# Unordered list scatters and a shift for the block count in a routed expert kernel

## The chip, the cores and the metric

The kernel runs on one core of a Trainium2 chip. The time is device microseconds from one launch, the median of several runs; lower is better. Engines are named as the profile names them: PE (matmul, with PEld for its weight loads), DVE (vector), ACT (scalar activation), POOL (GpSimd) and SP (which issues most DMAs).

## The reference, cut to what matters

4096 tokens of width 512 (two batches of 2048) pass through a linear-attention block and then a mixture of experts, each with a layer norm ahead and a layer norm and residual behind.

```python
x = x + layernorm(attn(layernorm(x)))            # 16 heads, 4 key heads, elu+1 features
def moe(x):                                      # 32 experts, width 192, 8 per token
    scores = softmax(x @ wg.T)
    weights, idx = top_k(scores, 8)
    weights = weights / weights.sum(-1)
    # every (token, expert) entry, sorted by expert:
    h = silu(xs @ w1[e]) * (xs @ v1[e])
    return zeros.at[token].add((h @ w2[e]) * weight)
x = x + layernorm(moe(layernorm(x)))
```

All arithmetic is in float32. 4096 tokens with 8 experts each give 32768 entries.

## The kernel before, in words

**Attention.** For each batch, the keys of 16 token tiles of 128 are reduced to a key state (`keys_of`), and then four blocks of 512 tokens run through `attn_block`. A finished block leaves four token tiles in a waiting list; `finish_next` takes one of them at a time, in between the work of the following block (or of the keys of the second batch), so each tile's residual, norm and routing run beside later attention matmuls. The last four tiles have no attention behind them; they are finished by the loop at L643, just ahead of the experts.

**Routing, `route_tile`.** For one tile of 128 tokens it computes the expert scores, the best eight (`top`), their weights, and for each of the eight a position in the expert's list: `carry` holds how many entries each expert has so far. `tw` (three buffers) holds token number and weight for each entry, `pi` (three buffers) the eight positions. L202 to L208 then issue eight indirect DMAs from POOL, one for each k; each scatters 128 entries of 8 bytes into `list_d` in device memory, which has room for 4096 entries for each expert. Every entry's row is written once. The list was filled with empty entries before by `clear_lists`. The framework that orders the program sees eight writes of the whole of `list_d` and makes each wait for the one before it to land. 32 tiles make 256 such DMAs.

**Two rounds of experts.** The lists are cut into blocks of 128 entries. Round 1 (48 blocks, 24 pairs) is planned after seven of the eight attention blocks, from the lists as they stand after 24 tiles. Round 2 takes the rest, up to 120 pairs; of these 114 run here. `plan_round` computes, with some forty small DVE operations on all 128 partitions, which expert and block each slot of a round holds, reads the blocks of the list by indirect DMA on POOL (L356: one for round 1, two for round 2), transposes them on PE, and leaves token numbers (`tid`), weights (`wt`) and expert numbers (`load`). For round 2 the number of pairs, `half`, is counted at L269 to L274: an iota of even numbers on POOL (`ev_i`), a copy, a comparison with the total number of blocks, and a sum. Its two list reads are held behind the matmul and scatter-add of round 1's pair 16 on their engines.

**A pair of blocks.** `prepare` loads the two experts' weights by SP (three buffers each; a load is skipped where the buffer already holds that expert), gathers the 128 tokens of each block by an indirect DMA on POOL (`xg`, L679, four buffers), transposes them on PE (L685) and copies them out on DVE (L687). `run_pair` multiplies with the first weights (L698), applies silu on ACT (`hs`, L701) and the product on DVE (`hh`, L702), transposes (L710), copies (`hT`, L712), multiplies with the second weights (`py`, L715 and L719), scales by the entry's weight on ACT into `ysb` (L723, three buffers), and adds the rows to `acc_d` by an indirect scatter-add on POOL (L724).

**What sets the order.** Every engine runs its own instruction list in order. The lists are written at build time by the framework's planner, which simulates the program and places an instruction when its inputs are ready; only SP keeps the order of the source in the expert rounds. A wait holds everything behind it on that engine. At the end, 16 steps add the two halves of `acc_d`, normalise, add the residual and store.

Of the kernel before, what the change touches and what calls it, by code (L numbers as in the profile page):

```python
# [9 lines left out]
I32 = mybir.dt.int32  # L10
U32 = mybir.dt.uint32
AF = mybir.ActivationFunctionType
ALU = mybir.AluOpType
AX = mybir.AxisListType
# [3 lines left out]
P = 128  # L18
# [5 lines left out]
def linear_attention_then_moe(  # L24
# [15 lines left out]
    nc = tc.nc  # L40
# [47 lines left out]
    list_d = dram.tile([E * CAP + BS, 2], F32, name="list_d")  # L88
# [30 lines left out]
    rn = ctx.enter_context(tc.tile_pool(name="rn", bufs=3))  # L119
# [7 lines left out]
    def transpose_rows(psum, dst, src):  # L127

        pt = psum.tile([P, C, P], F32, tag="pt", name="pt")
        for c in range(C):  # L130
            nc.tensor.transpose(pt[:, c, :], src[:, c * P : (c + 1) * P], ident)
        nc.vector.tensor_copy(dst, pt)
# [9 lines left out]
        return mv, rs  # L142

    carry = [None]

    def route_tile(i, xn):

        xnT = rn.tile([P, C, P], F32, tag="rn", name="xnT")
        transpose_rows(ps_r, xnT, xn)
        pl = ps_r.tile([P, E], F32, tag="pt", name="pl")  # L150
        for c in range(C):
            nc.tensor.matmul(pl, xnT[:, c, :], wg_sb[:, c, :], start=(c == 0), stop=(c == C - 1))
        nmx = sm.tile([P, 1], F32, tag="nmx", name="nmx")
        nc.vector.tensor_reduce(nmx, pl, AX.X, ALU.max, negate=True)
        sc = sm.tile([P, E], F32, tag="sc", name="sc")
        ssum = sm.tile([P, 1], F32, tag="ssum", name="ssum")
        nc.scalar.activation(sc, pl, AF.Exp, bias=nmx, accum_out=ssum)
        nc.vector.reciprocal(ssum, ssum)
        nc.vector.tensor_scalar_mul(sc, sc, ssum)

        top = sm.tile([P, K], F32, tag="top", name="top")
        nc.vector.max(top, sc)
        ti = sm.tile([P, K], U32, tag="ti", name="ti")
        nc.vector.max_index(ti, top, sc)
        e8 = sm.tile([P, K], F32, tag="e8", name="e8")
        nc.vector.tensor_copy(e8, ti)
        mk = sm.tile([P, E], F32, tag="mk", name="mk")
        nc.vector.match_replace(mk, top, sc, -1.0)
        nc.vector.tensor_single_scalar(mk, mk, 0.0, ALU.is_lt)

        pr = ps_r.tile([P, 2, E], F32, tag="pt", name="pr")
        nc.tensor.matmul(pr[:, 0, :], tri, mk, start=True, stop=True)
        nc.tensor.matmul(pr[:, 1, :], ones, mk, start=True, stop=True)

        tsum = sm.tile([P, 1], F32, tag="tsum", name="tsum")
        nc.vector.tensor_reduce(tsum, top, AX.X, ALU.add)
        nc.vector.reciprocal(tsum, tsum)
        tw = sm.tile([P, K, 2], F32, tag="tw", name="tw")
        nc.vector.tensor_copy(tw[:, :, 0], tok[:, i : i + 1].to_broadcast([P, K]))
        nc.vector.tensor_scalar_mul(tw[:, :, 1], top, tsum)  # L180

        before = ebase if carry[0] is None else carry[0]
        pos = sm.tile([P, E], F32, tag="pos", name="pos")
        nc.vector.tensor_add(pos, before, pr[:, 0, :])
        after = cy.tile([P, E], F32, tag="carry", name="after")
        nc.vector.tensor_add(after, before, pr[:, 1, :])
        carry[0] = after


        oh = sm.tile([P, K, E], F32, tag="oh", name="oh", bufs=2)  # L190
        nc.vector.tensor_tensor(
            oh,
            eidx.unsqueeze(1).to_broadcast([P, K, E]),
            e8.unsqueeze(2).to_broadcast([P, K, E]),
            ALU.is_equal,
        )
        nc.vector.tensor_mul(oh, oh, pos.unsqueeze(1).to_broadcast([P, K, E]))
        pos8 = sm.tile([P, K], F32, tag="pos8", name="pos8")
        nc.vector.tensor_reduce(pos8, oh, AX.X, ALU.add)
        pi = sm.tile([P, K], I32, tag="pi", name="pi")  # L200
        nc.vector.tensor_copy(pi, pos8)  # L201
        for k in range(K):  # L202
            nc.gpsimd.indirect_dma_start(  # L203
                out=list_d[:, :],
                out_offset=bass.IndirectOffsetOnAxis(ap=pi[:, k : k + 1], axis=0),
                in_=tw[:, k, :],
                in_offset=None,
            )  # L208

    def finish_tile(i, x1):  # L210

        rows = slice(i * P, (i + 1) * P)
        xr = rio.tile([P, HID], F32, tag="xr", name="xr")
        nc.sync.dma_start(xr, x[rows, :])
        nc.vector.tensor_add(x1, x1, xr)
        nc.sync.dma_start(x1_d[rows, :], x1)
        mv, rs = ln_stats(sm, x1)
        xn = rn.tile([P, HID], F32, tag="rn", name="xn")
        nc.vector.tensor_scalar(xn, x1, mv[:, 0:1], rs, ALU.subtract, ALU.mult)
        nc.sync.dma_start(xn_d[rows, :], xn)  # L220
        route_tile(i, xn)
# [32 lines left out]
    def plan_round(pool, nblk, offs, npair, gp, fixed, later=()):  # L254
# [6 lines left out]
        t = lambda name, w=ng: pool.tile([P, w], F32, name=name)  # L261
        incl = running_sum(pool, "incl", nblk)
        total = incl[:, E - 1 : E]
        half = t("half", 1)
        if fixed:
            assert fixed % 2 == 0
            nc.vector.memset(half, fixed / 2.0)
        else:
            evens = t("evens", npair)  # L269
            ev_i = rn.tile([P, npair], I32, tag="rn", name="ev_i")  # L270
            nc.gpsimd.iota(ev_i, [[2, npair]], base=0, channel_multiplier=0)
            nc.vector.tensor_copy(evens, ev_i)
            nc.vector.tensor_tensor(evens, evens, total.to_broadcast([P, npair]), ALU.is_lt)
            nc.vector.tensor_reduce(half, evens, AX.X, ALU.add)  # L274


        sec = t("sec", 1)
# [72 lines left out]
        lists = list_d.rearrange("(r f) o -> r (f o)", f=BS)  # L350
# [2 lines left out]
            order.enter_context(tc.issue_after(ins.ins))  # L353
        for g in range(ng):
            bl = rn.tile([P, BS, 2], F32, tag="rn", name="bl")
            nc.gpsimd.indirect_dma_start(  # L356
                out=bl[:n2].rearrange("p f o -> p (f o)"),
                out_offset=None,
                in_=lists,
                in_offset=bass.IndirectOffsetOnAxis(ap=row_i[:n2, g : g + 1], axis=0),  # L360
            )
            bt = rn.tile([P, 3, BS], F32, tag="rn", name="bt")
            nc.vector.tensor_copy(bt[:n2, :2, :], bl[:n2].rearrange("p f o -> p o f"))
            nc.vector.tensor_copy(bt[:n2, 2, :], ew[:n2, g : g + 1].to_broadcast([n2, P]))
            pt = ps_r.tile([P, 3, P], F32, tag="pt", name="pid")
            for o in range(3):
                nc.tensor.transpose(pt[:, o, :n2], bt[:n2, o, :], ident[:n2, :n2])
            nc.vector.tensor_copy(tid[:, g, :], pt[:, 0, :n2])
            nc.vector.tensor_copy(wt[:, g, :], pt[:, 1, :n2])
            nc.vector.tensor_copy(load[:, g, :], pt[:1, 2, :n2])  # L370
# [6 lines left out]
    with ExitStack() as actx:  # L377
# [243 lines left out]
        for b in range(B):  # L621
            acc = finish_kv(*keys)
            ms = fold_wo(acc)
            for t in range(NBLK):
                mid = attn_block(b, t, xls[t], acc, ms)
                if b == 0:
                    with tc.issue_after(mid):
                        clear_accumulators(t)
                if b * NBLK + t == SNAP:
                    nc.vector.tensor_sub(cnt1, carry[0], ebase)  # L630
                    full = blocks_of(route, "full", cnt1, BS - 1)
                    upto = running_sum(route, "upto", full)

                    f1 = route.tile([P, E], F32, name="f1")
                    nc.vector.tensor_sub(f1, full, upto)
                    nc.vector.tensor_scalar(f1, f1, float(N1), 0.0, ALU.add, ALU.max)
                    nc.vector.tensor_tensor(f1, f1, full, ALU.min)
                    round1 = plan_round(route, f1, None, NP1, NP1, N1)
            if b + 1 < B:
                keys = key_state()  # L640
                xls = keys_of(b + 1, *keys, lambda *_: finish_next())
# [5 lines left out]
    with ExitStack() as mctx:  # L647
# [90 lines left out]
        nblk = blocks_of(plan, "nblk", cnt, 0)  # L738
        nc.vector.tensor_sub(nblk, nblk, f1)
        round2 = plan_round(plan, nblk, f1, NP2, GP2, None, done[2 * NP1 // 3])  # L740
        np2 = plan.tile([P, 1], I32, name="np2")
        nc.vector.tensor_copy(np2, round2[3])
# [25 lines left out]
        for i in range(0, NTILE, 2):  # L768
            rows = slice(i * P, (i + 2) * P)
# [60 lines left out]
```

## Time and profile before

| | us |
|---|---|
| median of 3 runs | 2855.16 (2854.49 to 2856.72) |
| the profiled execution | 2861.29 |
| its span, first to last instruction | 2859.5 |
| attention, with the routing of 28 tiles | 0 to about 1335 |
| round 1, with the routing of the last four tiles | about 1335 to 1660 |
| round 2 | to about 2765 |
| closing norm and stores | to 2859.5 |

| engine | busy us | share |
|---|---|---|
| PE | 2645.8 | 93% |
| DVE | 1061.4 | 37% |
| POOL | 1059.9 | 37% |
| ACT | 674.8 | 24% |

A row of a timeline gives the start, the length, the engine, the line, the operation and its tiles, how many instructions were merged, and in brackets how long the engine had been idle and what ended that. "issue" means that the profile shows no wait. Busy time of POOL at a DMA is the time in which it prepares the transfer, not the transfer. A matmul's length follows the granted clock, which the rows by stretch give as a share of full speed.

The 256 list scatters (L203) keep POOL busy for 252.2 us, 985 ns each; POOL waits 365.8 us in 207 of them for the DMA of the scatter before.

### The profile page before, as it was taken

Reading aid. Unit: us, or ns where it says so; the run is one execution under the profiler, and the core shown is the slowest. Engines: PE = TensorE matmul, PEld = TensorE weight load, DVE = VectorE, ACT = ScalarE, POOL = GpSimd, SP = SyncE. Lnnn points to the kernel's source line nnn. Section 1 sums busy time; section 2 is a strip of 40 time slices with the busy share of each in tenths; the row PEclk is TensorE's granted clock in tenths of the full one; section 3 lists DMA queues with packets and bytes.
Section 4 is the critical chain, followed back from the end, with each engine's and each line's share of the span. In section 5 each row is a group of like instructions: output and inputs, shape, how many; then the busy total and the mean of one; then the engine's idle time right before and its main releaser. Section 6 shows DMA issues by size and latency. Waiting matters only on the chain. (4 is left out here: it accounts for less than half of the span.)

```text
span 2859.5 us, 29618 instructions
## 1 busy us (share of the span) xinstructions
PE 2645.8 (93%) x8443; PEld 1310.7 (46%) x8443; DVE 1061.4 (37%) x2432; ACT 674.8 (24%) x1208; POOL 1059.9 (37%) x891
## 2 busy tenths in 40 slices
PE   8999999998999999998779899999999999999850
PEld 3434444444444444444435455555555555555420
DVE  5334544546533536554412222222222222222217
ACT  4332222213331313221211112121212121212114
POOL 1100223122320122223455555555555555554426
PEclk9999999999999999999889999999999999999985
DMA  3291211212111212123647899989787988685548
GB/s 112 86 329 51 68 52 52 68 52 67 37 56 45 71 34 71 53 71 114 161 102 175 212 268 257 274 200 254 165 214 160 314 194 199 137 194 114 104 87 323
DMA packets 179290, 399.83 MB, mean 140 GB/s; under 512 B 29413, under 2 KB 30438, under 8 KB 178610
## 3 DMA queue, kind: packets, MB, share of 16 engines
q0 software_dynamic: 70144, 145.31, 25.1%
q1 hardware_dynamic: 101602, 237.55, 24.9%
q10 hardware_dynamic: 7376, 15.02, 1.4%
q8 instruction: 70, 1.15, 0.2%
q14 instruction: 98, 0.80, 0.1%
HBM read 488.74 MB, written 116.66 MB: 212 GB/s over the span
## 5 line engine op out<-in xcount | busy, mean ns | idle before, releaser
L698 PE MATMUL pgu<-w1t,xgT 128*128 128x384 f32 x2208 | 780.0, 496 | 3.5 <-issue 2.4
L724 POOL DMA_INDIRECT acc_d<-ysb,tid x276 | 441.9, 1601 | 503.8 <-ACT ysb L723 389.5
L203 POOL DMA_INDIRECT list_d<-tw,pi x256 | 252.2, 985 | 979.6 <-DVE pi L201 556.2
L698 PEld LDWEIGHTS pgu<-w1t,xgT 128*128 128x128 f32 x2208 | 399.5, 191 | 327.2 <-issue 109.3
L552 PE MATMUL pq<-xlT,wq_sb 128*128 128x512 f32 x1024 | 463.1, 598 | 1.2 <-DVE sq L559 1.2
L584 PE MATMUL acc<-m,sq 128*128 128x512 f32 x1024 | 463.0, 597 | 0.0
L702 DVE TENSOR_TENSOR hh<-hs,pgu 128x192 f32<-128x192 f32 x276 | 97.3, 355 | 975.9 <-ACT hs L701 838.2
L723 ACT ACTIVATE ysb<-py,wt 128x512 f32<-128x512 f32 x276 | 176.5, 684 | 783.4 <-PE py L719 731.8
L679 POOL DMA_INDIRECT xg<-xn_d,tid x276 | 274.9, 996 | 119.0 <-PE px L685 64.0
L552 PEld LDWEIGHTS pq<-xlT,wq_sb 128*128 128x128 f32 x1024 | 190.7, 190 | 241.5 <-issue 230.8
L584 PEld LDWEIGHTS acc<-m,sq 128*128 128x128 f32 x1024 | 189.1, 190 | 239.6 <-issue 239.1
L715 PE MATMUL py<-w2t,hT 128*128 128x512 f32 x552 | 266.4, 605 | 2.1 <-issue 2.1
L555 ACT ACTIVATE qe<-pq,nbq_sb 128x512 f32<-128x512 f32 x128 | 87.8, 686 | 514.6 <-PE pq L552 509.0
L687 DVE COPY xgT<-px 128x512 f32<-128x512 f32 x276 | 188.3, 683 | 43.6 <-PE px L685 41.3
L559 DVE SCALAR_TENSOR_TENSOR sq<-pq,bq_sb,qe 128x512 f32<-128x512 f32 x128 | 95.8, 748 | 286.0 <-ACT qe L556 285.9
L685 PE MATMUL px<-ident,xg 128*128 128x128 f32 x1104 | 174.2, 284 | 29.1 <-DMA xg<-xn_d,tid 26.7
L701 ACT ACTIVATE hs<-pgu 128x192 f32<-128x192 f32 x276 | 90.3, 330 | 363.2 <-PE pgu L698 336.7
L685 PEld LDWEIGHTS px<-ident,xg 128*128 128x128 f32 x1104 | 135.9, 147 | 56.9 <-issue 32.0
L715 PEld LDWEIGHTS py<-w2t,hT 128*128 128x128 f32 x552 | 107.5, 196 | 109.2 <-issue 74.0
L719 PE MATMUL py<-w2t,hT 64*128 64x512 f32 x552 | 157.1, 642 | 0.0
L710 PE MATMUL ph<-ident,hh 128*128 128x128 f32 x414 | 100.5, 298 | 51.3 <-DVE hh L702 51.2
L469 PE MATMUL pk<-wk_sb,xlT 128*128 128x512 f32 x256 | 119.7, 607 | 0.0
(185 smaller groups left out, 1844.8 us busy)
## 6 DMA issues: line engine op xcount, KB each, us to landing
w1t<-in_wgu_dram SPq DMA_DIRECT2D x276, 768.0 KB
w2t<-in_w2r_dram SPq DMA_DIRECT2D x276, 256.0 KB
w2t<-in_w2r_dram SPq DMA_DIRECT2D x276, 128.0 KB
nb<-nr_d SPq DMA_DIRECT2D x128, 256.0 KB
acc_d<-zero SPq DMA_DIRECT2D x6, 2048.0 KB
xb<-in_x_dram SPq DMA_DIRECT2D x32, 256.0 KB
xr<-in_x_dram SPq DMA_DIRECT2D x32, 256.0 KB
wo<-in_woT_dram SPq DMA_DIRECT2D x32, 256.0 KB
```

The lines of the kernel that those rows point to most:

```text
L203: nc.gpsimd.indirect_dma_start(out=list_d[:, :], out_offset=bass.IndirectOffsetOnAxis(ap=pi[:, k : k + 1], axis=0), in_=tw[:, k, :], in_of ...
L469: nc.tensor.matmul(pk, xlT[:, c, :], wk_sb[:, c, :], start=(c == 0), stop=(c == C - 1))
L552: nc.tensor.matmul(pq, wq_sb[:, c, h * P : (h + 1) * P], xlT[:, c, :], start=(c == 0), stop=(c == C - 1))
L584: nc.tensor.matmul(pa[s], a[:, s * P : (s + 1) * P], ms[h], start=(h == 0), stop=(h == H - 1))
L679: nc.gpsimd.indirect_dma_start(out=xg, out_offset=None, in_=xsrc, in_offset=bass.IndirectOffsetOnAxis(ap=tid[:, c0 : c0 + 1], axis=0),)
L685: nc.tensor.transpose(px[:, c, :], xg[:, c * P : (c + 1) * P], ident)
L687: nc.vector.tensor_copy(xgT, px)
L698: nc.tensor.matmul(pgu, xgT[:, c, :], w1t[:, c * F2 : (c + 1) * F2], start=(c == 0), stop=(c == C - 1))
L715: nc.tensor.matmul(py[s], hT[:, 2 * s, :], w2b[s][r][:, 0, :], start=True, stop=False)
L719: mm = nc.tensor.matmul(py[s], hT[rows, 1, :], w2b[s][r][rows, 1, :], start=False, stop=True)
L723: nc.scalar.activation(ysb, py[s], AF.Copy, scale=wt[:, c0 : c0 + 1])
L724: sc = nc.gpsimd.indirect_dma_start(out=acc_d[s][:, :], out_offset=bass.IndirectOffsetOnAxis(ap=tid[:, c0 : c0 + 1], axis=0), in_=ysb, in_ ...
```

## The change

Two things are changed.

The scatters into `list_d` are declared free of order among each other: each one is put into a group, and dependencies on members of that group are taken off the next. The three reads of the lists (L356) get an explicit dependency on every scatter issued before them in the program: 192 for round 1's read, 256 for each of round 2's.

For round 2, `half` is computed as (total + 1) shifted right by one bit, by three DVE operations on one column, in place of the iota on POOL and three DVE operations on 120 columns.

```diff
     carry = [None]
+    entries = []
...
         for k in range(K):
-            nc.gpsimd.indirect_dma_start(
+            sc = nc.gpsimd.indirect_dma_start(
                 out=list_d[:, :],
                 out_offset=bass.IndirectOffsetOnAxis(ap=pi[:, k : k + 1], axis=0),
                 in_=tw[:, k, :],
                 in_offset=None,
             )
+
+            tc.declare_no_dep(sc.ins, group="lists", reason="rows of list_d are set once")
+            tc.add_to_no_dep_group("lists", sc.ins)
+            entries.append(sc.ins)
...
         else:
-            evens = t("evens", npair)
-            ev_i = rn.tile([P, npair], I32, tag="rn", name="ev_i")
-            nc.gpsimd.iota(ev_i, [[2, npair]], base=0, channel_multiplier=0)
-            nc.vector.tensor_copy(evens, ev_i)
-            nc.vector.tensor_tensor(evens, evens, total.to_broadcast([P, npair]), ALU.is_lt)
-            nc.vector.tensor_reduce(half, evens, AX.X, ALU.add)
+            up = pool.tile([P, 1], I32, name="up")
+            nc.vector.tensor_scalar_add(up, total, 1.0)
+            nc.vector.tensor_single_scalar(up, up, 1, ALU.logical_shift_right)
+            nc.vector.tensor_copy(half, up)
...
-            nc.gpsimd.indirect_dma_start(
+            rd = nc.gpsimd.indirect_dma_start(
                 out=bl[:n2].rearrange("p f o -> p (f o)"),
                 out_offset=None,
                 in_=lists,
                 in_offset=bass.IndirectOffsetOnAxis(ap=row_i[:n2, g : g + 1], axis=0),
             )
+            for sc in entries:
+                tc.add_manual_dep(
+                    rd.ins, sc.name,
+                    mybir.DependencyInfo(mybir.DependencyClass.Sync, mybir.DependencyReason.DATA),
+                    reason="reads the lists",
+                )
```

## The prediction

> **What bounds the kernel now.** The chain of work that ended last covers only the closing normalisation (its shares are all near 0%), so I did not start there. I read, in order: the stretches of busy time by engine, the waits of PE, the timelines of PE, ACT, POOL and DVE around 1340 to 1510 us. PE is the busy engine (93% of the span), so a microsecond is worth something only where PE idles.
>
> Busy time by stretch (length, PE, weight loads, DVE, ACT, POOL, granted clock, DMA share, GB/s):
>
> ```profile
> 1340.00:1384.50 44.50, 39.09 (x160) 24.53 (x161) 27.59 (x113) 17.25 (x29) 16.26 (x14) 0.86 0.87 276
> 1384.50:1412.60 28.10, 12.43 (x35) 6.06 (x34) 9.86 (x46) 1.92 (x4) 13.99 (x13) 0.70 0.44 102
> 1412.60:1506.20 93.60, 67.01 (x211) 37.21 (x209) 15.24 (x34) 11.32 (x25) 49.36 (x45) 0.84 0.53 116
> 1506.20:1584.00 77.80, 77.08 (x274) 41.83 (x275) 18.98 (x40) 15.07 (x31) 42.40 (x33) 0.98 0.72 157
> ```
>
> A pair is 35 matmul records. The last row is round 1 undisturbed: L710 of successive pairs starts at 1527.07, 1536.90, 1546.73 us on PE, 9.83 us a pair. The second row does one pair in 28.1 us, the third six in 93.6 (15.6 a pair). That is where the list scatters of the last four token tiles (32 of the 256) run among the pairs. Between the start-up and 1300 us PE's matmuls wait under two microseconds at a time, but for 6.28 us at the batch change, behind a busy DVE.
>
> What holds the pairs, on POOL's timeline (start, length, idle before and releaser):
>
> ```profile
> 1413.37 0.98 POOL L203 DMA_INDIRECT list_d<-tw,pi  x1 [0.30 <-issue]
> 1421.92 0.98 POOL L203 DMA_INDIRECT list_d<-tw,pi  x1 [7.57 <-DMA list_d<-tw,pi]
> 1423.21 0.98 POOL L679 DMA_INDIRECT xg<-xn_d,tid  x1 [0.31 <-PE px L685]
> 1424.49 0.96 POOL L679 DMA_INDIRECT xg<-xn_d,tid  x1 [0.30 <-issue]
> 1425.75 1.00 POOL L203 DMA_INDIRECT list_d<-tw,pi  x1 [0.30 <-issue]
> 1428.56 0.97 POOL L203 DMA_INDIRECT list_d<-tw,pi  x1 [1.81 <-DMA list_d<-tw,pi]
> 1429.84 1.61 POOL L724 DMA_INDIRECT acc_d<-ysb,tid  x1 [0.30 <-issue]
> 1431.76 1.58 POOL L724 DMA_INDIRECT acc_d<-ysb,tid  x1 [0.30 <-issue]
> ```
>
> Each scatter waits for the scatter before it to land, here 7.57 and 1.81 us, and the in-order engine holds everything behind it. The scatter-add issued at 1429.84 had its data on ACT at 1419.21. ACT pays, then PE:
>
> ```profile
> 1427.78 0.69 ACT L723 ACTIVATE ysb<-py,wt 128x512 f32<-128x512 f32 x1 [4.78 <-PE py L719]
> 1435.03 0.69 ACT L723 ACTIVATE ysb<-py,wt 128x512 f32<-128x512 f32 x1 [6.56 <-DMA acc_d<-ysb,tid]
> 1435.61 0.54 ACT L701 ACTIVATE hs<-pgu 128x192 f32<-128x192 f32 x2
> ```
>
> ```profile
> 1427.68 4.78 PE L698 MATMUL pgu<-w1t,xgT 128*128 128x384 f32 x14
> 1436.38 0.47 PE L710 MATMUL ph<-ident,hh 128*128 128x128 f32 x1 [3.92 <-DVE hh L702]
> ```
>
> There are three ysb buffers, so the second copy of a pair needs the first scatter-add of the pair before to have landed (1429.84 to 1435.03, 5.2 us). Hence `hs`, `hh` and PE are late. At 1384 us there is a second form, on DVE:
>
> ```profile
> 1398.22 0.22 DVE L272 CAST evens<-ev_i 128x120 f32<-128x120 int32 x1 [13.44 <-POOL ev_i L271]
> 1398.36 0.35 DVE L702 TENSOR_TENSOR hh<-hs,pgu 128x192 f32<-128x192 f32 x1
> 1400.69 0.17 DVE L179 COPY tw<-tok 128x8 f32<-128x8 f32 x1 [1.99 <-DMA list_d<-tw,pi]
> ```
>
> The iota of round 2's plan sits on POOL behind scatters; DVE waits 13.44 us for it, with the pair's `hh` behind it, and PE idles 13.31.
>
> **Scatters without order.** Removed: the landing wait ahead of a scatter. Where nothing intervenes one scatter follows another every 2.37 us (0.97 busy, 1.40 wait); POOL's gathers, which do not wait for each other, follow every 1.27 (0.97 and 0.30). So 32 scatters cost 32 x 1.27 = 41 us of POOL, in bursts of eight (10.2 us), as each tile's `pi` is ready: 1359.8, 1370.6, 1377.6 us by the DVE timeline, the last near 1384. They can be over near 1404 us instead of 1501.9.
>
> *Six pairs, 1412.6 to 1506.2.* POOL then carries per pair two gathers (2 x 1.27) and two scatter-adds (2 x 1.91): 6.4 of 9.83 us. 93.6 - 6 x 9.83 = **34.6 us**.
>
> *The pair from 1384.4 to 1412.6.* It took 28.2, 18.4 over 9.83. How much returns depends on where the third scatter-add (first of the second pair, on ACT done by 1379.4) falls among the bursts, which the build decides and the trace cannot show. With none ahead: 18.4. With one burst, the first pair's two scatter-adds, then two bursts (1360.1 + 10.2 + 3.8 + 20.3): it issues at 1394.4, lands at 1399.6, while the copy that needs it would come at 1390.4: 9.2 late, of which some 2.5 us are slack (`hh` at 1420.45, `ph` at 1422.47 in the next, undisturbed pair, and 0.87 idle on ACT), so PE stalls 6.7. With three bursts it issues at 1404.6: a 17 us stall. With all four ahead even of the first scatter-add, the second copy of the pair before (1380.8) waits until some 1406: about 9 us worse than now. Ends: -9 and +18.4. I take two bursts, since the first scatter-adds become ready just as the first burst ends, and the third not until two more bursts are waiting.
>
> A stall also costs clock. After the 13.31 us wait `ph` x2 took 0.69 against 0.44, `pgu` x2 1.62 against 0.88, `py` 3.62 against 1.88 and 1.32 against 1.13: 2.9 us. [...] I take the row: 18.4 - 6.7 - 2.9 = **8.8 us**.
>
> [...] Then a burst would cost POOL next to nothing, and the sum would be 34.6 + 18.4 = 53. The 256 rows of 985 ns busy say otherwise; with them it is 43.4.
>
> *Elsewhere.* Token tiles beside attention: PE hides the scatters; DVE's `tw` waits of 3.2 and 3.7 us near 727 and 762 us each cost PE about 1.45, so 0 to 2.9. Against it, a burst may hold POOL's `sks` add for 10.2 us in the keys stage; `sk` has two buffers at about 7 us a tile, some 13 us of cover, 0 to -2. The first gathers of round 1 wait behind the last scatter at 1334.9, but attention's last matmuls also end there: 0 to 2. I take 0 for all three.
>
> **The shift.** Out: a POOL iota (0.24) and DVE's 0.22 + 0.28 + 0.28. In: three DVE operations on one column, 0.15 to 0.22 each by the plan's own one-column rows; the trace has no shift, but even doubled it is under 1.4 us. They hide beside PE as the plan's other thirty do. The 13.44 us wait goes, but alone it would buy little: next late is `tw` at 1400.69, whose buffer the first tile's scatters hold, and `hT` comes behind it in DVE's order. I count 0 beyond the sum above.
>
> **The wait on all scatters.** The list readers (L356) now name 192 or 256 scatters. At 17 ns for a semaphore row on POOL (x33 at L203) that is at most 4.4 us each, 8.8 for round 2's two; queued behind are the next pairs' gathers, and DVE's `bt`, which already holds `hh` for 9.23 us at 1593. At least it is 0, as all scatters have long landed. I take 0.1: the present reader also follows 256 scatters through one or a few semaphore values. That 7.4 us PE stall stays.
>
> **Sum.** 34.6 + 8.8 - 0.1 = 43.3 us. Against the profiled execution, 2861.3 (span 2859.5 and 1.8 around it), this gives 2818; that execution lies 6.1 above the median of the runs, so I predict 2855.2 - 43.3, **2812 us**.
>
> **Rivals.**
> - *Clean order* (0.25): the scatter-adds slip between scatters, 53 us and perhaps 3 from the `tw` waits: 2800. For it: the order of before also mixes both kinds. Against: eight scatters become ready at once.
> - *POOL becomes the bound for a while* (0.31): three or four bursts ahead of the scatter-adds, 34.6 - 1.3 to 34.6 - 9: 2822 to 2830.
> - *The waits do not go* (0.04), because another dependency keeps the order, or DVE's `tw` takes its place: the iota alone gives 0 to 2 us, 2854.
> - *Slower* (0.04): the scatters are put ahead of round 1's first gathers. These start at 1336.13; behind the fourth tile's burst they could start only near 1395, 59 us later with PE idle, against 53 recovered: 2861. It decides once the first gather starts after some 1389 us. Against: ten gathers stand ahead of these scatters today, since they are ready 24 us sooner.
>
> The likeliest case has 0.36. About 0.2% is what a measurement of this kernel can tell from no change: faster 0.92, within it 0.04, slower 0.04. The range takes in the first two rivals and the open terms: 2795 (53 + 2.9 + 2 + 2) to 2834 (34.6 - 9, less 4.4).
>
> **What would show it.** L203 spaced 1.27 us within a tile with no wait on its own DMA; the last scatter near 1404 us; no wait of ACT's ysb on acc_d of over 3 us after 1412; L710 every 9.83 us from then on; no evens row. PE's remaining stall before 1412 says which order was built. I am wrong if pairs stay above 10 us after the scatters end (then landing, not POOL, held them), or if attention grows.

## The result, and the profile after

The changed kernel takes 2883.4 us (median of 4 runs, 2873.8 to 2886.7) beside 2854.9 for the kernel before: a ratio of 1.0093, 95% interval 1.008 to 1.0107. It is slower by 0.9%, where 1.5% faster was forecast. The profiled execution has a span of 2884.8 us, 25.3 over that of before.

On POOL all that was forecast came. From the table of waits (us in all, times, longest), first before, then after:

```profile
POOL list_d L203 <- DMA list_d<-tw,pi: 365.8, 207, 7.6
...
DVE tw L179 <- DMA list_d<-tw,pi: 53.3, 13, 17.7
...
PE pn L567 <- DVE sq L559: 9.9, 9, 1.2
```

```profile
DVE tw L180 <- DMA list_d<-tw,pi: 218.2, 29, 11.7
...
PE pn L576 <- DVE sq L568: 30.6, 15, 3.6
...
POOL list_d L204 <- DMA list_d<-tw,pi: 1.2, 4, 0.3
```

POOL's 366 us are gone. But DVE now waits 218 us for the same scatters, at the copy of the token number into `tw` (L180), and PE's `pn` matmul waits three times as long for DVE as before. Both lie in attention (217 of the 218 us come before its last matmul at 1380.4), where the prediction had counted 0. Its stretch from 930 to 1330 us (the columns are those of the prediction's table), before and after:

```profile
930.00:1330.00 400.00, 394.14 (x1084) 173.31 (x1083) 204.51 (x515) 95.79 (x162) 92.45 (x94) 1.00 0.18 56
```

```profile
930.00:1330.00 400.00, 383.25 (x1018) 167.60 (x1017) 197.45 (x486) 95.27 (x158) 82.43 (x81) 0.96 0.17 56
```

In the same 400 us PE gets through 1018 matmul records and not 1084, with less busy time and at a lower granted clock (0.96). The last attention matmul starts at 1380.4 us and not at 1334.3. One such loss in the timeline after, a token tile's routing (`pi`, then eight scatters) beside attention:

```profile
993.65 0.17 DVE L202 CAST pi<-pos 128x8 int32<-128x8 f32 x1
994.10 0.97 POOL L204 DMA_INDIRECT list_d<-tw,pi  x1 [164.68 <-DVE pi L202]
995.37 0.97 POOL L204 DMA_INDIRECT list_d<-tw,pi  x1 [0.30 <-issue]
...
1003.65 0.97 POOL L204 DMA_INDIRECT list_d<-tw,pi  x1 [0.30 <-issue]
1005.87 0.17 DVE L180 COPY tw<-tok 128x8 f32<-128x8 f32 x1 [6.17 <-DMA list_d<-tw,pi]
1005.95 0.74 DVE L568 SCALAR_TENSOR_TENSOR sq<-pq,bq_sb,qe 128x512 f32<-128x512 f32 x1
...
1006.75 1.92 PE L576 MATMUL pn<-sq,kvacc 128*32 128x512 f32 x2 [3.35 <-DVE sq L568]
1008.60 2.08 PE L561 MATMUL pq<-xlT,wq_sb 128*128 128x512 f32 x2
```

The copy at 1005.87 is not for this tile but for the third one after it. It reads nothing of that tile, only a constant column, so the planner may place it as soon as a `tw` buffer is free, that is, when this tile's eight scatters have landed. By the order in which DVE ran its list, the copy stands 2 to 11 instructions behind the `pi` of the tile whose buffer it takes in 27 of 29 cases (the median is 6); before, where each scatter had to wait for the landing of the one ahead, it stood 7 to 71 behind (median 22). On the chip this burst takes 10.5 us (994.10 to 1004.62), and the copy, which waits for its landing, starts 1.25 us behind it. DVE reaches the copy at 999.7, waits 6.17 us, and holds `sq`, for which PE waits 3.35 us. Then `pn` x2 takes 1.92 us, where two took 1.04 at 985.54 behind a wait of 1.06, and `pq` x2 takes 2.08, where 28 took 12.26 just before (0.88 for two). The granted clock in the ten us behind the wait was 0.50:

```profile
1006.00:1016.00 10.00, 9.25 (x17) 4.41 (x18) 5.75 (x7) 0.00 (x0) 0.00 (x0) 0.50 0.08 28
```

Round 1 after, on ACT and PE:

```profile
1443.62 2.83 PE L707 MATMUL pgu<-w1t,xgT 128*128 128x384 f32 x8
1446.28 0.27 PE L719 MATMUL ph<-ident,hh 128*128 128x128 f32 x1
1446.39 2.75 PE L707 MATMUL pgu<-w1t,xgT 128*128 128x384 f32 x8
...
1455.50 0.33 ACT L710 ACTIVATE hs<-pgu 128x192 f32<-128x192 f32 x1 [9.77 <-remote]
1456.28 0.69 PE L719 MATMUL ph<-ident,hh 128*128 128x128 f32 x2 [7.14 <-DVE hh L711]
...
1463.40 0.33 ACT L710 ACTIVATE hs<-pgu 128x192 f32<-128x192 f32 x1 [7.57 <-remote]
1464.68 3.78 PE L724 MATMUL py<-w2t,hT 128*128 128x512 f32 x4 [5.16 <-DVE hT L721]
...
1471.64 0.27 PE L719 MATMUL ph<-ident,hh 128*128 128x128 f32 x1
...
1481.47 0.27 PE L719 MATMUL ph<-ident,hh 128*128 128x128 f32 x1
```

From 1471.64 on a pair comes every 9.83 us, as forecast. Ahead of it pairs are late in a new way. ACT's `hs` needs `pgu`, and by PE's rows the first eight `pgu` matmuls are done by 1446.5 and the next eight by 1449.2; yet ACT waits 9.77 and 7.57 us for PE's semaphore, until 1455.5 and 1463.4. The profile calls such a wait "remote": the semaphore changed, but no instruction that raises it had just ended. I call these unexplained waits. There are 53.6 us of them after (7.9 of these at 829 us, in attention), none before.

### The profile page after: what moved, and what is told of

The parts are those of the page before. It is cut to its first block, busy times and chain, and to the rows that moved or that the text cites. A ratio compares the mean times of both kernels' runs of the same rounds, so it can differ in the third digit from the quotient of the medians.

```text
span 2884.8 us, 29626 instructions
## 1 busy us (share of the span) xinstructions
PE 2662.9 (92%) x8443; PEld 1314.7 (46%) x8443; DVE 1059.0 (37%) x2432; ACT 682.6 (24%) x1213; POOL 1062.4 (37%) x890
## 5 line engine op out<-in xcount | busy, mean ns | idle before, releaser
L561 PE MATMUL pq<-xlT,wq_sb 128*128 128x512 f32 x1024 | 474.0, 609 | 2.4 <-DVE sq L568 2.3
L593 PEld LDWEIGHTS acc<-m,sq 128*128 128x128 f32 x1024 | 189.1, 190 | 239.7 <-issue 239.3
L694 PEld LDWEIGHTS px<-ident,xg 128*128 128x128 f32 x1104 | 133.1, 145 | 56.9 <-issue 31.3
L494 PE MATMUL gt<-sk,xl 128*128 128x512 f32 x256 | 118.0, 602 | 4.6 <-DVE sk L487 4.6
```

What stands on the lines that cost most here:

```text
L561: nc.tensor.matmul(pq, wq_sb[:, c, h * P : (h + 1) * P], xlT[:, c, :], start=(c == 0), stop=(c == C - 1))
L593: nc.tensor.matmul(pa[s], a[:, s * P : (s + 1) * P], ms[h], start=(h == 0), stop=(h == H - 1))
L694: nc.tensor.transpose(px[:, c, :], xg[:, c * P : (c + 1) * P], ident)
```

## The experiments

The measures in this table come from each profiled execution: DVE's waits for the scatters at `tw`; the start of the last attention matmul; the stage from the first `ph` to the `ph` that is held by round 2's list read (1594.49 before; 17 pairs lie between, 167 us at 9.83); and the sum of waits ended by "remote". The prediction's 43.4 us would have brought the stage to 199.4. Each ratio is against runs of before on the same chip, whose medians were 2851.2 to 2854.9.

| kernel | median us | ratio to before (95%) | tw | attention ends | stage | remote |
|---|---|---|---|---|---|---|
| before | 2854.9 | 1 | 53.3 | 1334.3 | 242.8 | 0 |
| after | 2883.4 | 1.0093 (1.0080 to 1.0107) | 218.2 | 1380.4 | 219.7 | 53.6 |
| e1: six tw buffers | 2878.1 | 1.0094 (1.0073 to 1.0114) | 196.3 | 1381.5 | 216.0 | 42.3 |
| e2: shift only | 2853.1 | 1.0002 (0.9994 to 1.0011) | 62.0 | 1333.1 | 239.7 | 2.2 |
| e3: scatters only | 2881.4 | 1.0113 (1.0097 to 1.0130) | 213.6 | 1371.5 | 220.0 | 45.6 |
| e4: before, six tw buffers | 2847.8 | 0.9985 (0.9976 to 0.9994) | 44.0 | 1331.1 | 232.9 | 0 |
| e5: after, tw from top | 2836.2 | 0.9938 (0.9925 to 0.9952) | 0 | 1336.9 | 216.6 | 30.6 |
| e6: before, tw from top | 2845.4 | 0.9977 (0.9969 to 0.9986) | 9.6 | 1328.8 | 236.3 | 0 |
| e7: last four tiles only | 2835.1 | 0.9943 (0.9929 to 0.9957) | 44.2 | 1332.6 | 216.3 | 27.2 |
| e8: e7, tw from top | 2827.3 | 0.9921 (0.9908 to 0.9935) | 0 | 1328.7 | 214.1 | 25.3 |
| e9: e6 without 32 scatters | 2803.8 | 0.9833 (0.9820 to 0.9847) | 0 | 1327.9 | 191.6 | 0 |
| e10: e8, half in order | 2822.1 | 0.9900 (0.9885 to 0.9915) | 6.0 | 1328.0 | 211.2 | 0 |
| e11: e8, at most five in flight | 2816.6 | 0.9877 (0.9862 to 0.9893) | 0.4 | 1327.4 | 206.9 | 0 |
| e12: e5, at most five in flight | 2822.2 | 0.9887 (0.9870 to 0.9905) | 0.4 | 1330.4 | 205.0 | 0 |
| e13: e7, at most five in flight | 2832.4 | 0.9926 (0.9912 to 0.9940) | 52.1 | 1333.2 | 216.5 | 16.3 |
| e14: after, at most five in flight | 2877.0 | 1.0087 (1.0074 to 1.0101) | 215.3 | 1380.3 | 212.9 | 29.7 |

**e1, six buffers for tw.**

```diff
-        tw = sm.tile([P, K, 2], F32, tag="tw", name="tw")
+        tw = sm.tile([P, K, 2], F32, tag="tw", name="tw", bufs=6)
```

> The changed kernel with six buffers for tw in place of three, so that DVE's copy into tw waits for scatters six tiles back. Theory (the copy into tw, placed in DVE's order right behind the burst, holds DVE for 6 to 11 us a tile and with it PE's pn): DVE's 218 us of waits for list_d at tw fall below 20, the last attention matmul comes back from 1380 to some 1335 to 1340 us, and the time falls by 25 to 45 us to 2838 to 2858 us. Rival 1 (the bursts of eight scatters on POOL hold something else, such as sks or the semaphores): the tw waits vanish too, but attention stays near 1380 and the time within 8 us of 2883. Rival 2 (another DVE wait takes the place of the one removed, half of it): 2860 to 2872.

Little changed, and the theory seemed to fall. But its premise had not been met. The waits of this kernel still have

```profile
DVE tw L180 <- DMA list_d<-tw,pi: 196.3, 26, 11.4
```

The copy has no input that ties it to its tile, so with six buffers the planner places tile i+6's copy behind tile i's burst instead of tile i+3's: in 25 of 26 cases it stands 2 to 11 instructions behind that tile's `pi`, as in the changed kernel, and 26 copies wait where 29 did. More buffers moved which copy blocks, not the block.

**e2, the shift alone; e3, the scatters alone** (each the change without its other half).

> The kernel before with the shift alone; the scatters stay in order. Theory (the shift is worth nothing beyond the iota's wait, and next late is tw): within 3 us of before, 2852 to 2858 us. Rival (the 13.4 us wait of DVE for the iota is worth its PE stall and clock): 2839 to 2845 us. Rival (the plan's moved operations stand worse): 2860 or more.

> The changed kernel with the counted columns back in place of the shift. Theory (the loss is that of the scatters alone): 2878 to 2892 us, attention's last matmul again near 1380 us. Rival (the shift gives part of the loss): below 2872. Rival (the iota behind bursts of scatters costs DVE more): above 2895.

The shift is worth nothing that can be measured, and the whole loss is in the scatters. In e2, `tw` is late at the iota's place (14.42 us at 1399.61), as the prediction had it.

**e4, the kernel before with six tw buffers.**

> The kernel before with six buffers for tw. Control for the first run: DVE's 53 us of tw waits vanish, of which few reach PE: theory 2848 to 2857 us. If the buffers alone gave 25 us or more (below 2832), the first run would say nothing about the change. Rival (DVE's later tw took pressure off POOL): slower by 3 us or more.

The time is at the edge of what was expected, 0.15% faster. But the waits at `tw` did not vanish, they fell from 53.3 to 44.0 us: here too the copies only moved back with the buffers. That more buffers alone are not worth 25 us stands.

**e5, tw tied to its own tile**, in the changed kernel; **e6**, the same edit in the kernel before.

```diff
-        nc.vector.tensor_copy(tw[:, :, 0], tok[:, i : i + 1].to_broadcast([P, K]))
+        nc.vector.tensor_scalar(tw[:, :, 0], top, 0.0, tok[:, i : i + 1], ALU.mult, ALU.add)
```

> The changed kernel; tw's token column is written as top times 0 plus the token number, so that the planner cannot place it before the tile's own routing. Six buffers had changed nothing because the copy has no other input: the planner put it behind the burst six tiles back instead of three. Theory (DVE's wait in the copy costs attention 46 us, stall and clock): DVE's 218 us at tw fall below 20, the last attention matmul comes back to 1333 to 1342 us, the time to 2830 to 2845 us. Rival (bursts hold attention in another way): last attention matmul above 1360, time above 2862. Rival (attention comes back but the pairs of round 1 lose what they had gained): 2848 to 2860.

> The kernel before with the same edit to tw alone. Control: its 53 us of DVE waits at tw vanish, two of which cost PE 1.5 us each. Theory: 2845 to 2854 us (six buffers gave 2848). Rival: below 2840, then the tw edit and not the scatters would make most of the gain of the run above.

This is the run that decides. The values are the same and DVE does the same number of instructions, but the copy now needs `top`. The waits of e5:

```profile
PE pn L576 <- DVE sq L568: 11.5, 9, 2.5
...
DVE tw L180 <- issue: 3.8, 21, 0.2
```

No wait of `tw` on `list_d` is left, PE's wait at `pn` is back near before's, attention ends at 1336.9 us, and the time falls by 47 us, to 0.6% under before (by the two ratios, each against its own chip, 44 us). The control e6 gains 0.2% by the same edit, so the tw edit is not itself the gain.

**e7, only the last four tiles without order; e8, that and tw from top.**

```diff
-            tc.declare_no_dep(sc.ins, group="lists", reason="rows of list_d are set once")
-            tc.add_to_no_dep_group("lists", sc.ins)
-            entries.append(sc.ins)
+            if i >= NTILE - 4:
+                tc.declare_no_dep(sc.ins, group="lists", reason="rows of list_d are set once")
+                tc.add_to_no_dep_group("lists", sc.ins)
+                entries.append(sc.ins)
```

> The changed kernel with the scatters of the last four tiles alone without order; those of the first 28 wait for each other as before. Theory (the loss is in attention, from the first 28 tiles' bursts and the tw copies behind them; the pairs' gain is from the last four): last attention matmul 1330 to 1345 us, time 2828 to 2845 us. Rival (a run of 16 to 32 scatters among the pairs costs by itself as much as the landing waits did): 2850 or more, with waits of ACT and DVE that no record explains between 1400 and 1470 us.

> The kernel of the run above with tw written from top as well. Theory (early tiles: order among scatters is worth nothing there): within 6 us of both e5_after_twdep and e7_last4, 2825 to 2842 us. Rival (unordered scatters are worth something beside attention too): e5_after_twdep faster than this by 8 us or more.

The theory holds: the loss is in the first 28 tiles' bursts, the gain in the last four. e8 is 8 to 9 us under both e7 and e5, where at most 6 were expected, so order among the first 28 tiles' scatters costs nothing once `tw` is tied. e5, without that order, ends attention 8 us later than e8; why, no run shows. But the stage is 214 to 216 us, not 199, and 25 to 27 us of unexplained waits are left.

**e9, without the last 32 scatters.**

```diff
-        for k in range(K):
+        for k in range(K if i < NTILE - 4 else 0):
```

> The kernel before with tw written from top; the 32 list scatters of the last four tiles are left out (their list entries stay empty, so round 2 gathers the padding row for them; the number of blocks and all else stay). It says what the 32 scatters cost in round 1 in all, beside 18 us that dropping their order gave (2845 to 2827). Theory (unordered, they still cost: 41 us of POOL in bursts, and semaphore updates that arrive late while they run; the three pairs before the 15 that lead to round 2's list took 67.5 us with them, some 30 to 45 would do without): 2795 to 2812 us. Rival (the start of round 1 is held by weights and gathers anyway, and the bursts cost nothing beyond): 2820 to 2828 us.

The time is within what was expected, and the stage is 191.6 us. Against e6, the 32 scatters in order cost 44.7 us of stage; without order (e8) they still cost 22.5.

**e10, half of the last tiles' scatters in order** (`i >= NTILE - 4 and k < 4` in e8).

> The kernel of e8_last4_twdep with only four of a tile's eight scatters free of order (last four tiles); the other four wait for the one before to land. Theory (back-to-back scatters are what delays semaphore updates and holds the three first pairs; half the density gives part of it back, while half of the landing waits come back): between the two, 2828 to 2840 us, with ACT's and DVE's waits on semaphores that no record explains below half of the 25 us of e8. Rival (landing waits alone count): 2834 to 2838 with the unexplained waits as before. Rival (the mix is best): below 2825.

The time is that of the third case, "the mix is best": 0.2% under e8, with intervals that just overlap, although landing waits came back (POOL's for `list_d` are 320.9 us in all, beside 313.4 in e8). The unexplained waits are gone.

**e11, e12, e13, e14: at most five in flight**, in e8, e5, e7 and the changed kernel. An odd scatter is declared free of order to the even one just before it, and to no other. In e11:

```diff
-            if i >= NTILE - 4:
-                tc.declare_no_dep(sc.ins, group="lists", reason="rows of list_d are set once")
-                tc.add_to_no_dep_group("lists", sc.ins)
+            if i >= NTILE - 4 and k % 2:
+                tc.declare_no_dep(sc.ins, group=f"lists{i}_{k}", reason="rows of list_d are set once")
+            elif i >= NTILE - 4:
+                tc.add_to_no_dep_group(f"lists{i}_{k + 1}", sc.ins)
+            if i >= NTILE - 4:
```

> The kernel of e8_last4_twdep in which each scatter of the last four tiles waits for the one some four places earlier; at 1.27 us a scatter those have landed, so the spacing stays and only the order in which the planner mixes them with gathers and scatter-adds changes. Theory (what counts is the spacing and the place among scatter-adds): within 6 us of e8, 2822 to 2833 us, unexplained waits 15 to 30 us. Rival (the number in flight delays the semaphores): unexplained waits below 8 us and 2812 to 2820 us.

> The changed kernel with tw written from top (as in e5_after_twdep), and in every tile a scatter from the sixth on waits for the one four places earlier, the next tile's first likewise, so that at most five are in flight; without that wait up to eight were. In e11 this went with waits on unexplained late semaphores falling from 25 us to 0, but the planner's mix of bursts and scatter-adds differed too. Theory (the number in flight beside the pairs' weight loads is what delays semaphores): in this other mix too the unexplained waits of e5 (30 us) fall below 8 us and the time to 2820 to 2830 us. Rival (e11 was luck of the mix): unexplained waits of 15 us or more, 2832 to 2840 us.

e11 is the fastest version that leaves nothing out, 1.2% under before, and e12 is 14 us under e5. Both times the unexplained waits are 0, as the number in flight would have it. POOL's timeline in e11:

```profile
1357.44 0.97 POOL L204 DMA_INDIRECT list_d<-tw,pi  x1 [0.30 <-issue]
1360.25 0.97 POOL L204 DMA_INDIRECT list_d<-tw,pi  x1 [1.85 <-DMA list_d<-tw,pi]
...
1363.12 0.96 POOL L204 DMA_INDIRECT list_d<-tw,pi  x1 [0.30 <-issue]
1364.39 1.60 POOL L736 DMA_INDIRECT acc_d<-ysb,tid  x1 [0.30 <-issue]
1366.30 0.99 POOL L204 DMA_INDIRECT list_d<-tw,pi  x1 [0.30 <-issue]
```

The new wait bites once: the sixth scatter waits 1.85 us, until the second of the tile has landed. Otherwise the spacing is still 1.27 us, and the planner has put scatter-adds and gathers after 8, 5, 3, 5, 3 and 8 scatters, where e8 has 8, 8, 8 and 8. So two things changed at once.

> The kernel of e7_last4 (tw as in the changed kernel, last four tiles without order) with at most five scatters in flight, as in e11 and e12. In those two the bursts were also cut shorter by scatter-adds and gathers in between; here the planner leaves a run of thirteen scatters. Theory (the number in flight counts, not how many stand in a row): waits on unexplained late semaphores 0 to 5 us in place of e7's 27, and 2815 to 2828 us in place of 2835. Rival (the length of the runs counts): unexplained waits 20 us or more, 2830 to 2842 us.

> The changed kernel with at most five scatters in flight in every tile and nothing else changed (tw's copy stays where the planner puts it). Theory (two independent losses): unexplained waits near 0 in place of 54 us, but DVE still blocked at tw for 150 us or more and the last attention matmul above 1365 us; 2855 to 2872 us. Rival (the tw waits come only from pile-ups): attention back below 1345, 2822 to 2835 us. Rival (nothing changes): 2878 or more.

In e13 and e14 the limit is the same, but thirteen scatters follow each other between two other transfers, and unexplained waits are back: 16.3 us in e13, between its theory and its rival, and 29.7 in e14 (11.8 of these in attention), whose time of 2877 us lies between its theory and "nothing changes". Of e13's waits:

```profile
ACT hs L713 <- remote: 7.8, 1, 7.8
...
DVE xgT L699 <- remote: 4.3, 1, 4.3
DVE hT L724 <- remote: 4.2, 1, 4.2
```

The number in flight alone therefore does not account for these waits. e14 also shows the two losses to be separate: fewer unexplained waits and a shorter stage by 7 us, attention as late as in the changed kernel.

## Why the prediction was wrong

By its own steps, in the two profiled executions (before less after, a gain positive):

| step | predicted | measured |
|---|---|---|
| attention, up to the first `ph` (1351.7; 1399.0) | 0 | -47.3 |
| the first three pairs, to the sixth `ysb` (57.0; 71.9 us) | +8.8 | -14.9 |
| 15 pairs from there, to the 36th `ysb` (192.5; 155.0) | +34.6 | +37.5 |

Their sum is -24.7, nearly all of the 25.3 us by which the span grew.

**The step that failed** is "Elsewhere": "PE hides the scatters", with 0 taken. It had seen both halves. It named `tw`'s waits on DVE and it had DVE's order behind `tw` at 1400.69, but it read them as waits that would go with the order. It took the place of the copy in DVE's list as given, while the place is the planner's answer to when the scatters land. Without the order the planner moved the copy up to where eight scatters are still being issued; in e7, where the first 28 tiles keep their order, the copies of attention stand where they stood before, 7 to 60 instructions behind. e5 shows what that cost: tied to its own tile, the copy no longer blocks, and 43.5 of attention's 46.1 us come back. The closing sentence, "I am wrong if ... attention grows", names what happened; "DVE's tw takes its place" stood among the rivals, but at 0 to 2 us of gain and in round 1 only.

**Size of that step.** In attention after, from 250 us on, PE's waits of over 1.2 us come to 31.3 us beside the 6.28 at the batch change, where before they were 4.2. That is 27 of 46. One of them, 4.23 us at 831.7, stands behind the unexplained wait at 829 and not behind `tw`. The rest I put down mainly to slower matmuls behind the waits: 383.25 us for 1018 records from 930 to 1330, 0.376 us each, against 0.364, is 13 us, and 376.41 for 1034 against 385.45 for 1067 from 270 to 660 is another 3. That makes 43 of the 46.

**The 8.8 us of the first pairs.** The order assumed (one burst, two scatter-adds, two bursts, then the third scatter-add) is that of e7, not of the changed kernel, where POOL issues 16 scatters in a row from 1404.68 to 1423.88 and then two scatter-adds. That is near the rival "POOL becomes the bound for a while". It does not explain the whole term: with the assumed order and an undisturbed attention, e7's stage still gives back only 26.5 of the 43.4 us, and 27.2 us of unexplained waits stand in that run. Without such waits (e11, e12) the stage is 205 to 207 us, near the 199.4 of the sum, and with them 212.9 to 220; e10, also without, has half of the last tiles' scatters in order again (7.5 us more of POOL's landing waits than e8) and stands at 211.2. The prediction had no term for such waits.

**What was right.** The 34.6 us for six pairs (37.5 measured over the longer stretch); 1.27 us from scatter to scatter; 9.83 us a pair afterwards; no "evens" row; nothing for the shift (e2); the list readers' wait (PE's stall there was 7.4 us and is 8.4). The last scatter came at 1461.2 instead of some 1404, 46 us of which are attention's. In e7, where attention is untouched, it came at 1409.0.

**What stays open.** Why semaphores are late. Counted between two other transfers of POOL, the longest run is 13 to 16 scatters in six kernels with unexplained waits of 16 us or more (after, e1, e3, e7, e13, e14). But it is eight in e5 and e8, which have such waits, eight in e11 and e12, which have none, and ten in e10, which has none. So no count of scatters in a row separates the two groups, and the length of a run was not varied alone.

Two more signs stand in the trace after and not in that of before. Register instructions of SP (`ALU_OP`, `MOVE`, `FUSED_REGOPS`) that take 0.55 to 0.80 us number 18 after, all between 1409 and 1457 us, and none before, where the median of the three kinds is 0.03 to 0.19. And semaphore records of the landings of POOL's transfers are fewer: from 1400 to 1500 us 312 beside 55 issues after, and 650 beside 47 before; in all, for 811 issues each, 9935 and 11615. That alone does not make a wait: before has 16 records an issue from 400 to 500 us (400 for 25) and 12.6 from 1600 to 1700 (542 for 43), and not one unexplained wait. Each run was recorded by the profiler, so the recording itself is not excluded: no run here tells it from a delay on the chip.

## What to carry to other kernels

A dependency that is removed changes two things: what the chip waits for, and what the planner believes; look in every engine's instruction list for what moved up behind the operation that is now thought to be quick, above all instructions with no input of their own step, such as a copy of a constant into a recycled buffer. Tie such an instruction to its own step (e5) rather than give it more buffers (e1). And drop order only where someone pays for it: here in 4 tiles of 32. That the version with its bursts broken up (e11) is the fastest is measured, not explained.

## What the runs showed of the hardware

- A scatter landed later beside the pairs' weight loads than beside attention. In the kernel before, where one scatter waits for the other, the wait beside attention is 1.4 us after the 0.97 us of issue (median of 189 waits before 1330; DMA share 0.18 from 930 to 1330), and 2.6 us (median of 16 waits from 1371 to 1496) among the pairs; at 1381.79, beside the loads, it is 4.99 (DMA share 0.87 from 1340 to 1384.5). In e11 the second scatter of a tile was issued at 1353.61, and the sixth, which waits for it, started at 1360.25, 6.6 us later. What else was in flight differs too, and no run separates it.
- A wait of PE of 2.45 us was followed by slower matmuls; the granted clock was 0.59 in the 4.2 us after it. In the timeline after, twelve `pq` records would take 5.3 us at the pace of the last line and took 6.18 (the row by stretch stands last):

```profile
1261.82 1.92 PE L576 MATMUL pn<-sq,kvacc 128*32 128x512 f32 x2 [2.45 <-DVE sq L568]
1263.66 6.18 PE L561 MATMUL pq<-xlT,wq_sb 128*128 128x512 f32 x12
...
1270.04 8.83 PE L561 MATMUL pq<-xlT,wq_sb 128*128 128x512 f32 x20
```

```profile
1261.80:1266.00 4.20, 4.18 (x6) 1.40 (x7) 2.50 (x5) 0.00 (x0) 0.00 (x0) 0.59 0.00 0
```
